# The edge stage of a four-layer graph network: an order written out by hand, loads of five blocks, edges loaded first

## The chip, the cores and the metric

The kernel runs on one NeuronCore of a Trainium2 chip. A core has engines that run side by side, each with its own queue of instructions: TensorE (PE; its weight loads are shown as PEld), VectorE (DVE), ScalarE (ACT), GpSimd (POOL) and SyncE (SP), which here only issues DMAs. DMAs move data between the device's memory (DRAM) and the on-chip memories SBUF and, through an engine, PSUM. An engine takes its instructions in the order of its queue and waits at each one until the data and buffers that it needs are there. The metric is the device time of one execution in microseconds (us), the median of several.

## What is computed

A graph has N = 3125 nodes with 128 features and E = 103125 directed edges (src, dst), sorted by dst. Four graph layers follow one another; each is added to its input and normalised.

```python
x = layernorm(x + relu(segment_sum(edge_weight[:, None] * (x @ W0)[src], dst) + b0))     # layer 0
x = layernorm(x + GAT(x, src, dst))                   # layer 1: attention, 4 heads of 32
x = layernorm(x + (x + edge_softmax(x) @ Wo))         # layer 2: attention with Q, K, V over the edges
x = layernorm(x + sigmoid(SAGE2(relu(SAGE1(x)))))     # layer 3: two mean aggregations
```

The change concerns only what stands before and within layer 0.

## The kernel before

The kernel turns the edge list into two dense tables in DRAM and then works with matrix products. `wd` (3200 x 3200, float32) holds for every pair (node, source) the sum of its edge weights, and `f_ctd` (25 x 128 x 3200, bfloat16) the number of its edges. Nodes are counted in blocks of P = 128, of which there are NB = 25.

**Before the edge stage.** Lines 577 to 642 load dst, src and the weights, compute a sort key of each edge, write a table `td` of keys, local sources and weights to DRAM (L634), and find for each *window* where its edges begin (`row_i`, L641). A window is five nodes (WN = 5); there are NW = 640 windows, in NG = 5 groups of 128. The features x are loaded on SP (L643, L645), and the weights and biases of all layers on ACT's queue (`load`, L541, and L714). Then an indirect DMA a group on GpSimd (L649) fetches 256 edges for each of the group's windows.

**Keys.** `keys_of(g)` (L655 to L695) turns a group's edges so that the edges of a window lie on the partitions, and writes the keys as bfloat16 pairs (`kd2`, `kc2`) and the weight as three bfloat16 parts (`w2`), the third one being also kept in float32 (`wu`). Groups 0 and 1 are done before the stage, the others within it, all at one place (in `make`, at block 8g - 6).

**The edge stage** (L855 to L904) runs over NBT = 40 blocks of BW = 16 windows. For each block

- `make(b)` lets DVE compare keys with a ramp, which gives two one-hot matrices `ohd` and `ohc` (L827), and multiply `ohd` by the weight parts, which gives three `wod` (L836); half of the third is made on ACT (L845), four windows at a time. `make(b + 1)` is called while block b is in work; `ohd`, `ohc` and `wod` have two buffers each.
- For four windows at a time PE makes `cp`, the counts (8 products, L867), and `wp`, the sums of weights (24 products, L875); ACT copies them to `cs` (L880) and `ws` (L886). `cp` and `wp` share three PSUM buffers.
- SP stores `ws` to `wd` (L888), 80 node rows a block, and every second block `cs` to `f_ctd` (L891), 160 node columns.

**Layer 0's products.** `add0` (L787 to L800) loads 128 rows of `wd` by 10 blocks of 128 columns (640 KB, `cw`, three buffers) and multiplies each block by `xw = x @ W0`, summing into five PSUM banks for the first Z0 = 20 blocks of sources (L797). One such product is here called an *add*; the trace has two records for each. There are 25 x 20 = 500 adds. They are queued as soon as the rows that they need have been stored a block earlier. The last five blocks of sources follow after the stage, in other PSUM banks.

What sets the order: nothing is written out by hand in this part. The framework's scheduler fills each engine's queue by readiness and by the order of the code, so adds, copies and key steps move to where it finds room.

Of the kernel before, what the change touches and what calls it, by code (L numbers as in the profile page):

```python
# [7 lines left out]
F32 = mybir.dt.float32  # L8
BF16 = mybir.dt.bfloat16
# [483 lines left out]
BW = 16  # L493
KW = WN * NB
NBT = NW // BW
Z0 = 20
V1 = 100
GA = 80.0
# [10 lines left out]
def fast_path(  # L509
# [28 lines left out]

    def load(name, ap, shape):
        t = cst.tile(shape, F32, name=name)  # L540
        nc.scalar.dma_start(t, ap)  # L541
        return t

    def row(name, v, n):
# [30 lines left out]
    with ExitStack() as st:  # L575
# [64 lines left out]
        nc.vector.tensor_scalar(cnt, cnt, 1.0, 0.0, OP.subtract, OP.max)  # L640
        nc.vector.tensor_scalar(row_i, cnt, float((P * ER - EW) // 16), None, OP.min)  # L641
        nc.vector.tensor_copy(ramp, ramp_i)
    nc.sync.dma_start(x[:, 0:NF, :], x_in[0 : NF * P, :].rearrange("(b p) d -> p b d", p=P))  # L643
    nc.gpsimd.memset(x[:, NF, :], 0.0)
    nc.sync.dma_start(x[0:NR, NF, :], x_in[NF * P : N, :])  # L645
    egs = []
    for g in range(NG):
        eg = ep.tile([P, EW // 16, 3, 16], F32, name="eg", bufs=3)
        nc.gpsimd.indirect_dma_start(  # L649
            out=eg.rearrange("p a t k -> p (a t k)"), out_offset=None, in_=td,  # L650
            in_offset=bass.IndirectOffsetOnAxis(ap=row_i[:, g : g + 1], axis=0),
        )
        egs.append(eg)

    def keys_of(g):  # L655

        eg = egs[g]
        kd2 = kp.tile([P, P // BW, 2, BW, 2], BF16, name="kd2")
        kc2 = kp.tile([P, P // BW, 2, BW, 2], BF16, name="kc2")
        w2 = [kp.tile([P, P // BW, 2, BW, 2], BF16, name=f"w2_{s}") for s in range(3)]  # L660
        kic = ep.tile([P, EW], F32, name="kic", bufs=2)
        nc.vector.tensor_scalar(
            kic.rearrange("p (a k) -> p a k", k=16), eg[:, :, 0, :], thr[:, g : g + 1], None, OP.subtract
        )

        nc.vector.memset(kic[:, EW - 1 : EW], -1.0)
        kid = ep.tile([P, EW], F32, name="kid", bufs=2)
        nc.vector.tensor_copy(kid.rearrange("p (a k) -> p a k", k=16), eg[:, :, 1, :])
        wei = ep.tile([P, EW], F32, name="wei", bufs=2)
        nc.scalar.copy(wei.rearrange("p (a k) -> p a k", k=16), eg[:, :, 2, :])  # L670
        t0 = cps.tile([P, 4, P], F32, name="t0", tag="cw")
        t1 = cps.tile([P, 2, P], F32, name="t1", tag="cw")
        for h in range(2):
            a = slice(h * P, (h + 1) * P)
            nc.tensor.transpose(t0[:, h, :], kid[:, a], ident)
            nc.tensor.transpose(t0[:, 2 + h, :], kic[:, a], ident)
            nc.tensor.transpose(t1[:, h, :], wei[:, a], ident)

        def each(i, h):
            return i[:, h, :].rearrange("p (b w) -> p b w", w=BW)  # L680

        def pairs(i, h):
            return each(i, h)[:, :, :, None].to_broadcast([P, P // BW, BW, 2])

        wt = ep.tile([P, 2, P], F32, name="wt", bufs=2)
        wu = kp.tile([P, 2, P], F32, name="wu")
        for h in range(2):
            copy(kd2[:, :, h, :, :], pairs(t0, h))
            copy(kc2[:, :, h, :, :], pairs(t0[:, 2:, :], h))
            nc.scalar.copy(w2[0][:, :, h, :, :], pairs(t1, h))  # L690
        for s, (i, o) in enumerate(((t1, wt), (wt, wu))):
            for h in range(2):
                nc.vector.tensor_tensor(each(o, h), each(i, h), w2[s][:, :, h, :, 0], OP.subtract)
                nc.scalar.copy(w2[s + 1][:, :, h, :, :], pairs(o, h))
        return kd2, kc2, w2, wu  # L695

    keys = {0: keys_of(0), 1: keys_of(1)}


    l0_wt = load("f_l0_wt", l0_w, [P, P])  # L700
    l0_br = cst.tile([P, P], F32, name="l0_br")
    nc.gpsimd.memset(l0_br, 0.0)
    nc.scalar.dma_start(l0_br[0:1, :], l0_b.rearrange("(o k) -> o k", o=1))
# [7 lines left out]
    nc.gpsimd.memset(att, 0.0)  # L711
    for s, a in enumerate((l1_as, l1_ad)):
        for h in range(H):
            nc.scalar.dma_start(att[h * C : (h + 1) * C, s * H + h : s * H + h + 1], a[h, :].rearrange("(c o) -> c o", o=1))  # L714
    wqt = load("f_wq", l2_wq, [P, P])
    wkt = load("f_wk", l2_wk, [P, P])
    wvt = load("f_wv", l2_wv, [P, P])
# [7 lines left out]
    watt = cst.tile([P, 2 * H], F32, name="watt")  # L725
    wyv = cst.tile([P, 2 * P], F32, name="wyv")
    both = cst.tile([P, P], F32, name="f_both")
    def products_of_weights():
        nc.gpsimd.tensor_tensor(both, gb_row, sb_row, OP.add)
        tw = {}  # L730
        for name, w in (("l1", l1_wt), ("q", wqt), ("k", wkt), ("v", wvt)):
            t = zps.tile([P, P], F32, name="trw", tag="acc3")
            nc.tensor.transpose(t, w, ident)
            tw[name] = ep.tile([P, P], F32, name="tw_" + name)
            nc.scalar.copy(tw[name], t)
        t = zps.tile([P, P], F32, name="trw", tag="acc3")
        nc.tensor.matmul(t[:, 0 : 2 * H], tw["l1"], att, start=True, stop=True)
        nc.scalar.copy(watt, t[:, 0 : 2 * H])
        t = zps.tile([P, P], F32, name="trw", tag="acc3")
        nc.tensor.matmul(t, tw["q"], tw["k"], start=True, stop=True)  # L740
        nc.scalar.copy(wyv[:, 0:P], t)
        t = zps.tile([P, P], F32, name="trw", tag="acc3")
        nc.tensor.matmul(t, tw["v"], wot, start=True, stop=True)
        nc.scalar.copy(wyv[:, P:], t)
# [39 lines left out]
        for j in range(n):  # L784
            nc.tensor.matmul(acc[:, j, :], ones, l0_br, start=(j == 0), stop=False, skip_group_check=True)

    def add0(pool, i, accs, blocks):  # L787

        b0, n = blocks
        for h in range(0, n, 10):  # L790
            m = min(10, n - h)
            cw = pool.tile([P, min(10, n), P], F32, name="cw")[:, 0:m]
            nc.sync.dma_start(
                cw.rearrange("p c d -> p (c d)"), wd[i * P : (i + 1) * P, (b0 + h) * P : (b0 + h + m) * P]
            )
            for j in range(h, h + m):
                nc.tensor.matmul(  # L797
                    accs[j // 4][:, j % 4, :], cw[:, j - h, :], xw[:, i, :], start=False,
                    stop=(i == NB - 1 and (j % 4 == 3 or j == n - 1)), skip_group_check=True,
                )  # L800

    def end0(acc, b0, n):
        t = lp0.tile([P, 4, P], F32, name="r0")
# [2 lines left out]
        )  # L806
        layer_norm(lp0, x[:, b0 : b0 + n, :], t, (0, n), True)

    zp = front.enter_context(tc.tile_pool(name="f_zp", bufs=3))
    sp = front.enter_context(tc.tile_pool(name="f_stg", bufs=2))  # L810
    SB = 2
    wv_ = wd.rearrange("(w i) (c d) -> w (i c) d", i=WN, d=P)

    def make(b):

        if b % 8 == 2 and 8 < b < NBT - 8:
            keys[b // 8 + 1] = keys_of(b // 8 + 1)
        kd2, kc2, w2, w3 = keys[b // 8]
        ohd = op_.tile([P, 2 * BW, P], BF16, name="ohd")
        ohc = op_.tile([P, 2 * BW, P], BF16, name="ohc")  # L820
# [1 line left out]
        def twos(k):  # L822
            k = k[:, b % 8, :, :, :].rearrange("p q w t -> p (q w) t")
            return k[:, :, None, :].to_broadcast([P, 2 * BW, P // 2, 2])

        for o, k in ((ohd, kd2), (ohc, kc2)):
            nc.vector.tensor_tensor(  # L827
                o.rearrange("p w (a t) -> p w a t", t=2), twos(k),
                ramp.rearrange("p (a t) -> p a t", t=2)[:, None, :, :].to_broadcast([P, 2 * BW, P // 2, 2]),
                OP.is_equal,  # L830
            )
        wod = []
        for s in range(3):
            f = of_.tile([P, 2 * BW, P], BF16, name="wod")
            n = 2 * BW if s < 2 else BW
            nc.vector.tensor_tensor(  # L836
                f[:, 0:n].rearrange("p w (a t) -> p w a t", t=2), ohd[:, 0:n].rearrange("p w (a t) -> p w a t", t=2),
                twos(w2[s])[:, 0:n], OP.mult,
            )
            wod.append(f)  # L840

        def more(k):
            for w in range(k, k + 4):
# [4 lines left out]

    cs = None
    acc0 = None  # L850
    done = 0
    cur = make(0)
    for k in range(0, BW, 4):
        cur[3](k)
    for b in range(NBT):  # L855
        ohd, ohc, wod, _ = cur
        cur = make(b + 1) if b + 1 < NBT else None
        if b % SB == 0:
            cs = sp.tile([P, NB, SB * BW * WN], BF16, name="cs")
        ws = sp.tile([P, BW, P], F32, name="ws")  # L860
        for k in range(0, BW, 4):
            cp = cps.tile([P, 4, P], F32, name="cp", tag="cw")
            wp = cps.tile([P, 4, P], F32, name="wp", tag="cw")
            for j in range(4):
# [16 lines left out]
                cs[:, :, i0 : i0 + 4 * WN].rearrange("p c (w i) -> p c w i", i=WN),  # L881
                cp[:, :, 0:KW].rearrange("p w (i c) -> p c w i", c=NB),
            )
            if cur:
                cur[3](k)
            nc.scalar.copy(ws[:, k : k + 4, :], wp)  # L886
        for a, e in ((0, 112), (112, KW)):
            nc.sync.dma_start(wv_[b * BW : (b + 1) * BW, a:e, :].rearrange("w k d -> k w d"), ws[a:e, :, :])  # L888
        if b % SB == SB - 1:
            i0 = (b - SB + 1) * BW * WN  # L890
            nc.sync.dma_start(ctd[:, :, i0 : i0 + SB * BW * WN].rearrange("c d i -> d c i"), cs)  # L891
        if b < 2:
            for blocks in GB[4 * b : 4 * b + 4]:
                xw_of(*blocks)
        if b == 2:
            products_of_weights()
            acc0 = [zps.tile([P, 4, P], F32, name=f"acc{k}", tag=f"acc{k}") for k in range(Z0 // 4)]
            for a in acc0:
                bias0(a, 4)
        while acc0 and (done + 1) * P <= (b - 1) * BW * WN:  # L900
            add0(zp, done, acc0, (0, Z0))
            done += 1
    for i in range(done, NB):
        add0(zp, i, acc0, (0, Z0))  # L904
    front.close()
    r = xw

# [770 lines left out]
```

## Time and profile before

| | us |
|---|---|
| median of 3 runs | 1528.68 (1528.14 to 1530.35) |
| the profiled execution | 1528.75 |
| its span, from the first to the last instruction | 1526.9 |
| busy in the span: PE, DVE, ACT, POOL | 1391.9, 985.8, 910.6, 126.8 |

The stages in the span: up to about 43 us loading, the table and the first keys; to 469 us the edge stage; to 499 us the last adds of layer 0; then the rest of layer 0 and layer 1 to about 970, layer 2 to about 1251 and layer 3 to the end. A busy PE counts the modelled length of pipelined products and so overstates what it works. Shares over the whole span mix these stages; the edge stage has to be read by itself.

In the page's part 2 each digit is the busy share of one fortieth of the span in tenths. The edge stage is slices 1 to 12 there:

```profile
PE   4899999999997987899989989899999999999994
PEld 3898999998997876889979979677777764458994
DVE  4999899999990489879978888544464451012006
ACT  2988778888882479878778677554465431023003
```

### The profile page before, as it was taken

The page shows a single profiled execution, that of the slowest core. Times are in us where ns is not written, and L with a number is a line of the kernel's source. Part 1 is how long each engine was busy: PE and PEld are TensorE (multiplying, and loading weights), DVE is VectorE, ACT ScalarE, POOL GpSimd, SP SyncE. Part 2 cuts the span into 40 slices and gives each one's busy share as a digit, 9 for nine tenths or more (in the row PEclk, how much of TensorE's full clock was granted, in tenths as well). Part 3 has the DMA queues.
Part 4 walks back from the last instruction along what each step waited for, and adds up shares of the span by engine and source line. Part 5 has one row for each costly group of instructions (what it writes and reads, how often), then busy time and mean ns, then how long its engine had stood idle before and what let it go on. Part 6 is the DMA issues. An engine that isn't in the chain of part 4 may idle for free. (4 is left out here: it accounts for less than half of the span.)

```text
span 1526.9 us, 35224 instructions
## 1 busy us (share of the span) xinstructions
PE 1391.9 (91%) x14858; PEld 1220.9 (80%) x14871; DVE 985.8 (65%) x1608; ACT 910.6 (60%) x1865; POOL 126.8 (8%) x162
## 2 busy tenths in 40 slices
PE   4899999999997987899989989899999999999994
PEld 3898999998997876889979979677777764458994
DVE  4999899999990489879978888544464451012006
ACT  2988778888882479878778677554465431023003
POOL 2000000000000023203212311300000000000000
PEclk9999999999998999999999999999999999999997
DMA  6387787887878633444434433332222227503551
GB/s 193 88 216 212 208 228 206 236 211 208 222 211 247 207 96 99 145 123 122 129 121 116 130 89 104 101 111 68 73 64 80 69 89 259 200 22 151 196 174 45
DMA packets 210337, 223.92 MB, mean 147 GB/s; under 512 B 72860, under 2 KB 183975, under 8 KB 209913
## 3 DMA queue, kind: packets, MB, share of 16 engines
q1 hardware_dynamic: 206312, 217.26, 48.4%
q10 hardware_dynamic: 3457, 2.35, 0.6%
q8 instruction: 118, 1.93, 0.5%
q0 software_dynamic: 400, 1.97, 0.4%
q14 instruction: 50, 0.41, 0.1%
HBM read 157.19 MB, written 64.36 MB: 145 GB/s over the span
## 5 line engine op out<-in xcount | busy, mean ns | idle before, releaser
L1244 PE MATMUL acc<-vp,cm 128*128 128x198 bf16 x2500 | 344.5, 252 | 6.6 <-DVE cm L1229 4.1
L1228 ACT ACTIVATE fm<-adr,bas 128x896 bf16<-128x896 f32 (+1 forms) x320 | 286.2, 952 | 67.9 <-DVE cm L1229 63.3
L1239 PE MATMUL acc<-vp,ct 128*128 128x204 bf16 x1250 | 315.2, 256 | 9.7 <-DVE vp L1147 5.6
L1244 PEld LDWEIGHTS <-cm 128*128 128x128 bf16 x2500 | 235.8, 98 | 25.9 <-issue 10.4
L875 PE MATMUL wp<-wod,ohc 128*128 128x128 bf16 x3840 | 244.1, 219 | 8.8 <-ACT cs L880 6.6
L875 PEld LDWEIGHTS <-ohc 128*128 128x128 bf16 x3840 | 224.0, 98 | 9.8 <-issue 9.4
L836 DVE TENSOR_TENSOR wod<-ohd,w 128x4096 bf16<-128x4096 bf16 (+1 forms) x120 | 224.9, 1926 | 0.6 <-PE wp L875 0.6
L1229 DVE TENSOR_TENSOR cm<-fm,ct 128x896 bf16<-128x896 bf16 (+1 forms) x320 | 197.5, 647 | 36.3 <-PE acc L1244 13.2
L845 ACT ACTIVATE wod<-ohd,wu 128x128 bf16<-128x128 bf16 x640 | 197.0, 400 | 0.0
L1384 DVE TENSOR_TENSOR e<-e,ct 128x416 f32<-128x416 f32 (+1 forms) x175 | 108.2, 625 | 106.5 <-ACT e L1383 98.6
L1383 ACT ACTIVATE e<-s,f_nm 128x416 f32<-128x416 f32 (+1 forms) x175 | 109.5, 632 | 98.1 <-PE s L1380 90.8
L1388 PEld LDWEIGHTS acc<-self__8127,e 128*128 128x128 f32 x1250 | 148.4, 193 | 20.6 <-issue 18.8
L1388 PE MATMUL acc<-self__8127,e 128*128 128x129 f32 x1250 | 148.8, 276 | 0.5 <-DVE e L1384 0.5
L1380 PE MATMUL s<-yT,f_xT 128*128 128x416 f32 (+1 forms) x350 | 142.8, 543 | 4.6 <-ACT rt L1360 4.0
L797 PE MATMUL acc<-f_xw,cw 128*128 128x128 f32 x1000 | 119.8, 280 | 7.2 <-DMA cw<-wd 7.2
L1239 PEld LDWEIGHTS <-ct 128*128 128x128 bf16 x1250 | 122.5, 98 | 2.5 <-issue 1.5
L886 ACT COPY ws<-wp 128x512 f32<-128x512 f32 x160 | 93.5, 584 | 49.9 <-PE wp L875 48.3
L797 PEld LDWEIGHTS acc<-f_xw,cw 128*128 128x128 f32 x1000 | 116.3, 196 | 7.5 <-DMA cw<-wd 7.3
L867 PE MATMUL cp<-ohc,ohd 128*128 128x125 bf16 x1280 | 96.8, 218 | 21.0 <-ACT ws L886 17.4
L1380 PEld LDWEIGHTS s<-yT,f_xT 128*128 128x128 f32 x350 | 62.2, 191 | 55.5 <-issue 39.2
L827 DVE TENSOR_TENSOR ohd<-kd,ramp 128x4096 bf16<-128x4096 bf16 x40 | 91.4, 2286 | 21.2 <-PE cp L867 21.1
L1562 PEld LDWEIGHTS <-ct 128*128 128x128 bf16 x1875 | 104.9, 98 | 0.0
(292 smaller groups left out, 1490.3 us busy)
## 6 DMA issues: line engine op xcount, KB each, us to landing
ct<-f_ctd SPq DMA_DIRECT2D x49, 800.0 KB
wd<-ws SPq DMA_DIRECT2D x40, 896.0 KB
ct<-f_ctd SPq DMA_DIRECT2D x150, 224.0 KB
cw<-wd SPq DMA_DIRECT2D x50, 640.0 KB
f_ctd<-cs SPq DMA_DIRECT2D x20, 1000.0 KB
ct<-f_ctd SPq DMA_DIRECT2D x25, 416.0 KB
ct<-f_ctd SPq DMA_DIRECT2D x25, 365.2 KB
cw<-wd SPq DMA_DIRECT2D x25, 320.0 KB
```

The source lines that it names most:

```text
L797: nc.tensor.matmul(accs[j // 4][:, j % 4, :], cw[:, j - h, :], xw[:, i, :], start=False, stop=(i == NB - 1 and (j % 4 == 3 or j == n - 1)) ...
L836: nc.vector.tensor_tensor(f[:, 0:n].rearrange("p w (a t) -> p w a t", t=2), ohd[:, 0:n].rearrange("p w (a t) -> p w a t", t=2), twos(w2[s] ...
L845: nc.scalar.activation(wod[2][:, BW + w, :], ohd[:, BW + w, :], AF.Copy, scale=w3[:, 1, at : at + 1])
L875: nc.tensor.matmul(wp[:, j, :], ohc[:, w, :], wod[s][:, w, :], start=(j == 0 and q == 0 and s == 0), stop=(j == 3 and q == 1 and s == 2), ...
L1228: nc.scalar.activation(f[:, : n * P], at, AF.Relu, bias=bas[:, c, h : h + 1], scale=UP)
L1229: nc.vector.tensor_tensor(m[:, : n * P], f[:, : n * P], ct[:, : n * P], OP.min)
L1239: nc.tensor.matmul(out_(F1, PW), ct[:, k * P : (k + 1) * P], vp[:, c, hp : hp + 2, :, 2 * F1 : V1], start=(c == 0), stop=False, skip_group ...
L1244: nc.tensor.matmul(out_(0, 2 * F1)[:, j], ms[j][:, k * P : (k + 1) * P], vp[:, c, hp + j, :, 0 : 2 * F1], start=False, stop=(c == NB - 1 a ...
L1380: nc.tensor.matmul(s[:, :m], xT[:, c * P : (c + 1) * P], yT[:, i0 * P + a : i0 * P + a + m], start=True, stop=True)
L1383: nc.scalar.activation(e[:, a : a + m], s[:, :m], AF.Exp, bias=nm[:, q : q + 1], scale=scale)
L1384: nc.vector.tensor_tensor(e[:, a : a + m], e[:, a : a + m], ct[:, a : a + m], OP.mult)
L1388: nc.tensor.matmul(acc[k // 3][:, (k % 3) * (P + 1) : (k % 3 + 1) * (P + 1)], es[q, c][:, k * P : (k + 1) * P], vo[:, c, 0 : P + 1], start ...
```

## The change

It does the following.

- The last block has 4 windows instead of 16 (LW = 4): 628 windows are the first to cover 3125 nodes. The 60 rows of `wd` that no window writes any more are set to zero by six stores from a tile `none`, and the end of the last `cs` by a memset.
- Until the table `td` is stored, only edges (and layer 0's weight and bias) are loaded. x is loaded behind the second indirect DMA, and all other weights behind x, on SP's queue instead of ACT's.
- `keys_of` becomes `key_steps`, seven steps. For group 0 they run at once; those of group g + 1 run in the blocks 8g to 8g + 6, one a block. The turned keys go from PSUM to SBUF first (`k_`, `w_`).
- From block 3 on, the order of PE, DVE, ACT and SP is that of the code (`manual_schedule`). After each four windows 3 or 4 adds from a list follow.
- `adds5` loads 5 blocks of columns at a time (320 KB, ZB = 6 buffers). A block's loads are issued behind its own stores of `ws`, for rows that were stored a block earlier, and its store of `cs` behind the loads.

```diff
+LW = 4
+NL = (NBT - 1) * BW + LW
+Z5 = 5
+ZB = 6
...
     def load(name, ap, shape):
         t = cst.tile(shape, F32, name=name)
-        nc.scalar.dma_start(t, ap)
+        with tc.issue_after(x_load.ins):
+            nc.sync.dma_start(t, ap)
         return t
...
-    nc.sync.dma_start(x[:, 0:NF, :], x_in[0 : NF * P, :].rearrange("(b p) d -> p b d", p=P))
-    nc.gpsimd.memset(x[:, NF, :], 0.0)
-    nc.sync.dma_start(x[0:NR, NF, :], x_in[NF * P : N, :])
...
+        if g == 1:
+
+            with tc.issue_after(got.ins):
+                nc.gpsimd.memset(x[:, 0:1, 0:1], 0.0)
+                nc.gpsimd.memset(x[:, NF, :], 0.0)
+    x_load = nc.sync.dma_start(x[:, 0:NF, :], x_in[0 : NF * P, :].rearrange("(b p) d -> p b d", p=P))
...
+        def turn():
+            t = cps.tile([P, 4, P], F32, name="t", tag="cw")
+            for h in range(2):
+                nc.tensor.transpose(t[:, h, :], kid[:, h * P : (h + 1) * P], ident)
+                nc.tensor.transpose(t[:, 2 + h, :], kic[:, h * P : (h + 1) * P], ident)
+            nc.scalar.copy(k_, t)
...
+        def twice():
+            for h in range(2):
+                nc.scalar.copy(kd2[:, :, h, :, :], pairs(k_, h))
+                nc.vector.tensor_copy(kc2[:, :, h, :, :], pairs(k_[:, 2:, :], h))
+                nc.scalar.copy(w2[0][:, :, h, :, :], pairs(w_, h))
...
+        return [
+            columns, turn, twice, lambda: less(0, w_, wt), lambda: part(1, wt), lambda: less(1, wt, wu),
+            lambda: part(2, wu),
+        ]
...
+    def adds5(k):
+
+        i, h = divmod(k, Z0 // Z5)
+        cw = zp.tile([P, Z5, P], F32, name="cw")
+        nc.sync.dma_start(
+            cw.rearrange("p c d -> p (c d)"), wd[i * P : (i + 1) * P, h * Z5 * P : (h + 1) * Z5 * P]
+        )
+        return [
+            lambda j=j: nc.tensor.matmul(
+                acc0[(h * Z5 + j) // 4][:, (h * Z5 + j) % 4, :], cw[:, j, :], xw[:, i, :], start=False,
+                stop=(i == NB - 1 and (h * Z5 + j) % 4 == 3), skip_group_check=True,
+            )
+            for j in range(Z5)
+        ]
...
-    zp = front.enter_context(tc.tile_pool(name="f_zp", bufs=3))
+    zp = front.enter_context(tc.tile_pool(name="f_zp", bufs=ZB))
...
     for b in range(NBT):
+        if b == 3:
+
+            order = ExitStack()
+            order.enter_context(
+                tc.manual_schedule(
+                    engines={mybir.EngineType.PE, mybir.EngineType.DVE, mybir.EngineType.Activation, mybir.EngineType.SP}
+                )
+            )
         ohd, ohc, wod, _ = cur
         cur = make(b + 1) if b + 1 < NBT else None
+        nw = BW if b < NBT - 1 else LW
+        if b % 8 == 0 and b < NBT - 8:
+            steps = key_steps(b // 8 + 1)
+        at = b % 8 if b < NBT - 8 else 7
...
             nc.scalar.copy(ws[:, k : k + 4, :], wp)
+            m = min(4 if k == 4 else 3, len(todo))
+            for f in todo[:m]:
+                f()
+            del todo[:m]
+            added += m
+            if k == 4 and at in (1, 2, 4, 6):
+                steps[{1: 1, 2: 2, 4: 4, 6: 6}[at]]()
...
-        if b % SB == SB - 1:
-            i0 = (b - SB + 1) * BW * WN
-            nc.sync.dma_start(ctd[:, :, i0 : i0 + SB * BW * WN].rearrange("c d i -> d c i"), cs)
...
-        while acc0 and (done + 1) * P <= (b - 1) * BW * WN:
-            add0(zp, done, acc0, (0, Z0))
-            done += 1
-    for i in range(done, NB):
-        add0(zp, i, acc0, (0, Z0))
+
+        while b > 2 and (loads // (Z0 // Z5) + 1) * P <= b * BW * WN and loads < added // Z5 + ZB:
+            todo += adds5(loads)
+            loads += 1
+        if b % SB == SB - 1:
+            i0 = (b - SB + 1) * BW * WN
+            nc.sync.dma_start(ctd[:, :, i0 : i0 + SB * BW * WN].rearrange("c d i -> d c i"), cs)
+    order.close()
+    for f in todo:
+        f()
+    while loads < NB * Z0 // Z5:
+        for f in adds5(loads):
+            f()
+        loads += 1
```

## The prediction

> **What bounds the kernel now.** I read the windows view first, cut at the borders of the edge stage, because shares over the whole span mix five stages. Block 3's last copy out of PSUM ends at 84.5 us and block 39's last edge product at 468.9.
>
> ```profile
> core 0: us, PE busy (x) PEld busy (x) DVE busy (x) ACT busy (x) POOL busy (x), PEclk, DMA share, GB/s
> 84.50:469.00 384.50, 358.91 (x5444) 353.70 (x5441) 354.48 (x204) 317.99 (x875) 0.05 (x1) 1.00 0.81 216
> 469.00:499.20 30.20, 22.44 (x170) 21.93 (x170) 3.71 (x23) 2.25 (x4) 1.40 (x2) 0.83 0.71 212
> 0.00:43.27 43.27, 19.62 (x116) 17.23 (x117) 22.38 (x47) 15.98 (x45) 7.68 (x19) 1.00 0.58 171
> 43.27:84.50 41.23, 36.98 (x571) 35.34 (x571) 41.23 (x21) 38.43 (x111) 0.00 (x0) 1.00 0.50 133
> ```
>
> In the long row PE (359 us) and DVE (354) are both near the stage's 384, ACT is at 318 and the DMA engines at 0.81: there is no single bound, and each engine idles some 25 to 30 us, by turns. The waits view of that stretch says on whom.
>
> ```profile
> PE cp L867 <- ACT ws L886: 17.4, 12, 1.6
> ...
> DVE ohd L827 <- PE cp L867: 21.1, 16, 1.7
> ```
>
> No product waits for a DMA there. Then the timeline, for the price of one step and for the tail (start, duration, engine, operation).
>
> ```profile
> 436.60 0.60 PE L867 MATMUL cp<-ohc,ohd 128*128 128x125 bf16 x8
> ...
> 438.38 0.60 PE L867 MATMUL cp<-ohc,ohd 128*128 128x125 bf16 x8
> ...
> 470.74 9.30 PE L797 MATMUL acc<-f_xw,cw 128*128 128x128 f32 x80
> 473.59 3.23 SPq L888 DMA_DIRECT2D wd<-ws  x2
> 476.87 1.57 SPq L891 DMA_DIRECT2D f_ctd<-cs  x1
> 478.55 22.81 SPq L793 DMA_DIRECT2D cw<-wd  x9
> ...
> 487.19 11.92 PE L797 MATMUL acc<-f_xw,cw 128*128 128x128 f32 x80 [7.16 <-DMA cw<-wd]
> ```
>
> Four windows (8 cp and 24 wp products) take 438.38 - 436.60 = 1.78 us. 80 records are 40 adds of a 128x128 block, so one add is about 9.1/40 = 0.226 us. DVE's five operations of a block repeat every 9.94 us when nothing stops them (ohd at 440.88, the next at 450.82). The tail shows PE standing 7.16 us for a load.
>
> Last the DMA queue, in windows in which it moved one kind each: a store of wd, a store of f_ctd, loads of cw.
>
> ```profile
> DMA packets 2004, 1.02 MB, mean 237 GB/s; under 512 B 87, under 2 KB 2003, under 8 KB 2003
> ...
> DMA packets 3165, 1.02 MB, mean 204 GB/s; under 512 B 3098, under 2 KB 3165, under 8 KB 3165
> ...
> DMA packets 371, 1.23 MB, mean 350 GB/s; under 512 B 30, under 2 KB 143, under 8 KB 371
> ```
>
> So wd takes about 4 us of the queue per block, f_ctd 5 us per two blocks, and a load of 320 KB 0.95 us.
>
> **What the Trainium skill says.** "DMA: Bandwidth & Descriptors", section Queues, rings and completion order: on one issuing engine's ring, descriptors are consumed in order. The trace agrees: in the tail the load issued at 478.55 released PE only at 487.19, behind a wd and an f_ctd store. Same page, Issuing engines are not separate DMA queues: moving an issue from ACT to SP saves issue time only; before, a weight's issue costs ACT 0.44 us (the row at 8.71). "TensorE: Matmul & The Clock Gate", section HAM oscillation: PE gaps over about 3.4 us while a DMA is awaited bring the clock back to half. The trace agrees: after the 7.16 us gap 80 records took 11.92 us instead of 9.30, at a mean clock of 0.83.
>
> **The change, part by part.**
>
> *Twelve windows fewer.* Block 39 has 4 windows of 16: PE saves 3 x 1.78 = 5.3 us, DVE about 7 of its 9.94. Six stores of zeros (0.77 MB, some 3 us of queue) replace them early, beside compute: nothing.
>
> *Fixed order.* From block 4 each group of 4 windows carries 3 or 4 adds, 13 a block. PE per block: 4 x 1.78 + 13 x 0.226 = 10.06 us. DVE: 9.94 plus about 2.4 us of keys per 8 blocks = 10.24. ACT: four times (cs 0.47, four scalings 1.29, ws 0.47) = 8.9, with keys 9.5. The slots fit. Blocks 4 to 39 need of PE 35 x 7.12 + 1.78 + 449 adds x 0.226 + 3 key turns x 1.3 = 356 us, where before took 384. I leave 3 us for frictions: -25 us. With frictions as before (28) it would be 0; with none -28.
>
> *Loads behind the stores.* I followed the code's counters, which the instruction order of the changed program confirms on PE and SP. A load of row i is queued at the end of the first block b with 128(i+1) <= 80b, after block b's own wd store, and its adds stand in PE's queue in the order of the loads. 80 node rows a block bring 12.5 adds, 13 are spent, so the list runs dry. The first load of a batch is then used in the first slot of the next block (loads 0, 44, 52, 60, 64, 72, 80, 84), in the second (24, 32, 40) or in the third (4, 12, 20, 48, 68, 76, 88).
> PE ends block b at B. The last ws copy ends at B + 0.5 (cs, scalings and ws stand on ACT behind the last cp). The load lands L after that store's issue. L from the tail: 487.19 - 473.59 = 13.6, less 5.0 for the f_ctd store between them, less 0.95 because that load was twice as large: 7.7. Landing B + 8.2. PE reaches the first slot's adds at B + 1.8, the second's at B + 4.25, the third's at B + 6.9. Waits: 8 x 6.4 = 51, 3 x 4.0 = 12, 7 x 1.3 = 9, in all 72 us. Later loads of a batch land 0.95 us apart and five adds last 1.1 us, so they wait for nothing more. Before, the scheduler put adds where the data was there. Queued behind the waiting add on PE are the next cp and wp; ACT waits for those, and DVE, one block ahead, waits for cp. PE and DVE are equally loaded, so the wait is lost for both; only where DVE is late anyway is some of it covered. I take 66 (bounds 30, if L were 5 us, and 80, if the f_ctd store of the block before still fills the queue).
>
> *The clock after such a wait.* 8 waits of over 3.4 us; the trace's one example cost 11.92 - 9.30 = 2.6 us. 8 x 2.6 = 21; I take 16 (bounds 0 and 28, the latter with the 4 us waits).
>
> *Key steps.* The same operations in seven places, with two more copies on ACT (k_ and w_, some 1 us a group, in its 9.5); DVE's 2.4 us a group is in the sum. PE's turn is 12 records, 1.3 us, in the sum. The groups' stalls of before (three of 3 us) are in the 25.
>
> *Start.* Before, the table's store at 13.6 shared the queue with x, which lands at 19.39, and the first gather started at 23.27. Without x and weights I put the gather at 17.5, and DVE's first make is some 6 us earlier. But ACT was busy 38.4 of 41.2 us in blocks 0 to 3 already, and all of f_xw's 14 copies (0.5 us each) and group 1's first key copies now fall there, some 50 us of ACT work after the first keys at about 31. Block 3 ends at about 82 instead of 84.5: -2.5 (bounds +4 and -8). SP's 26 weight loads and six stores of zeros go ahead of the first wd store: 34 issues x 0.44 = 15 us from 20, before that store is ready at 45: nothing; if they ran late, ACT's third ws would wait, 5 us at most.
>
> *Tail.* From the last edge product, the quarter store, three loads (2.9), the last f_ctd store (5.1), five loads (4.8) and the landing come to about 20, with the last adds 21, where before took 30.2: -9 (bounds -4 and -13). What follows has the same instruction order as before on all engines: 0.
>
> Sum: -25 + 66 + 16 - 2.5 - 9 = +45.5 us. The profiled execution took 1528.75 us (span 1526.9), practically the median 1528.68: 1528.7 + 45 = **1574 us**.
>
> **The rivals.** *Faster: the loads are hidden.* If DVE paces the stage (10.24 us a block against PE's 10.06) and PE reaches the first slot late, or a load lands within 2 us of its slot, no wait is left: -25 - 2.5 - 9 = -37, 1492 us. For it: today's queue is free for a fifth of the time and no load holds PE within the stage. Against: those adds were placed when the data was there. It decides where waits and clock together stay below 37 us, a mean first-slot wait under about 3.5 us. *Half-hidden:* loads 3 us sooner: 8 x 3.5 + 3 = 31 of waits, clock 6: 1529, between 1513 and 1545. *Worse:* each wait also lets the f_ctd store of the pair collide with the next batch, and every wait over 3.4 us costs the clock two periods: waits 80, clock 28: 1600. That the change does not do what it says is excluded by the instruction order: the adds stand where the code puts them.
>
> **How the numbers follow.** Likeliest, as summed, 0.63 (own range 1548 to 1594); hidden 0.16; half-hidden 0.13; worse 0.08. The range reaches down to 1500 into the hidden case, up to 1594, and leaves out some 0.11 below and 0.06 above. About 0.2% is what a measurement of this kernel can tell from no change. Faster: 0.16 + 0.05 = 0.21; same 0.03; slower 0.76.
>
> **What would show it.** In the profile after, the add's line should have idle time before it released by "DMA cw<-wd", some 60 to 70 us in about 11 long waits, most of them from block 20 on; PEclk under 1.0 in the second half of the stage; the stage from block 4 to 39 near 441 us; the gather before 19 us; the tail near 21 us. No such idle time, and a stage under 365 us, would prove the forecast wrong; waits of 2 to 3 us would mean that L was mis-sized.

## The result and the profile after

The changed kernel takes 1582.63 us (median of 4, 1581.79 to 1582.88) where the kernel before, beside it on the same chip, takes 1529.07 (1528.14 to 1530.35): a ratio of 1.0351, 95% interval 1.0339 to 1.0363. It is 3.5% slower, 8.6 us above the forecast of 1574 and within its range.

From the page of the changed kernel: its span, the busy times, and the group of the adds (busy us, mean ns of one, then the idle time of the engine ahead of them and what ended it).

```profile
span 1581.1 us, 35138 instructions
...
PE 1410.5 (89%) x14775; PEld 1238.9 (78%) x14775; DVE 980.0 (62%) x1613; ACT 912.8 (58%) x1857; POOL 141.3 (9%) x164
...
L857 PE MATMUL acc<-f_xw,cw 128*128 128x128 f32 x1000 | 155.3, 298 | 67.0 <-DMA cw<-wd 66.8
```

The same group on the page of the kernel before:

```profile
L797 PE MATMUL acc<-f_xw,cw 128*128 128x128 f32 x1000 | 119.8, 280 | 7.2 <-DMA cw<-wd 7.2
```

The adds have 67 us of idle PE ahead of them instead of 7, all but 0.2 of it ended by a load of `wd`. The windows view of the changed kernel, cut near the end of block 3 and at 531.5, about one us before the last edge product ends (the columns are those of the prediction's first fence), says where:

```profile
36.07:88.00 51.93, 47.22 (x639) 44.57 (x638) 45.00 (x31) 48.10 (x138) 13.79 (x2) 1.00 0.46 120
88.00:531.50 443.50, 383.52 (x5388) 377.76 (x5386) 347.48 (x208) 319.44 (x868) 1.35 (x1) 0.93 0.74 191
531.50:556.00 24.50, 17.09 (x139) 16.52 (x136) 4.06 (x25) 3.09 (x6) 1.45 (x2) 0.86 0.84 226
```

The long stretch grew from 384.5 to 443.5 us. PE is busy for 384 of them, the DMA engines are less busy than before (0.74 instead of 0.81), and the granted clock is 0.93 instead of 1.00. The waits view of the stretch from 88 to 532 us (us in total, times, longest):

```profile
ACT cs L972 <- PE cp L959: 115.2, 113, 7.9
DVE ohd L895 <- PE cp L959: 86.3, 29, 8.6
PEld acc L857 <- DMA cw<-wd: 63.2, 18, 7.3
PE acc L857 <- DMA cw<-wd: 59.8, 17, 7.1
```

ACT and DVE wait for PE, and PE waits for the load. One such wait in the timeline, at the end of a block:

```profile
289.90 0.60 PE L959 MATMUL cp<-ohc,ohd 128*128 128x125 bf16 x8
290.34 1.50 PE L967 MATMUL wp<-wod,ohc 128*128 128x128 bf16 x24
290.51 3.21 SPq L987 DMA_DIRECT2D wd<-ws  x2
293.83 2.21 SPq L853 DMA_DIRECT2D cw<-wd  x4
297.68 1.65 PE L857 MATMUL acc<-f_xw,cw 128*128 128x128 f32 x6 [5.83 <-DMA cw<-wd]
299.11 1.05 PE L959 MATMUL cp<-ohc,ohd 128*128 128x125 bf16 x8
299.95 2.09 PE L967 MATMUL wp<-wod,ohc 128*128 128x128 bf16 x24
```

The block's store of `ws` is issued at 290.51, the loads behind it from 293.83 on, and the adds of the next block's first slot start at 297.68 (a slot is the products of four windows and the adds behind them; a block has four). PE has done that slot's products at about 291.8 and stands for 5.83 us. After the wait the same 8 and 24 products take 1.05 and 2.09 us instead of 0.60 and 1.50, for the clock is at half until 301.2.

The difference, taken at the ends of PE's products (so that the stretches add up):

| | before | after | difference |
|---|---|---|---|
| last product of block 3 | 82.9 | 87.0 | +4.1 |
| from there to the last edge product | 385.9 | 445.6 | +59.7 |
| from there to the last add of the tail | 30.3 | 22.9 | -7.4 |
| the rest | 1027.8 | 1025.6 | -2.2 |
| span | 1526.9 | 1581.1 | +54.2 |

### The profile page after: what moved, and what is told of

It reads as the page before. It is cut to its first block, busy times and chain, and to the rows that moved or that the text cites. A ratio compares the mean times of both kernels' runs of the same rounds, so it can differ in the third digit from the quotient of the medians.

```text
span 1581.1 us, 35138 instructions
## 1 busy us (share of the span) xinstructions
PE 1410.5 (89%) x14775; PEld 1238.9 (78%) x14775; DVE 980.0 (62%) x1613; ACT 912.8 (58%) x1857; POOL 141.3 (9%) x164
## 5 line engine op out<-in xcount | busy, mean ns | idle before, releaser
L967 PE MATMUL wp<-wod,ohc 128*128 128x128 bf16 x3768 | 247.4, 224 | 1.8 <-ACT k__328 L699 1.6
L967 PEld LDWEIGHTS <-ohc 128*128 128x128 bf16 x3768 | 228.1, 101 | 2.6 <-issue 2.0
L906 DVE TENSOR_TENSOR wod<-ohd,w 128x4096 bf16<-128x4096 bf16 (+2 forms) x122 | 221.1, 1868 | 0.0
L857 PE MATMUL acc<-f_xw,cw 128*128 128x128 f32 x1000 | 155.3, 298 | 67.0 <-DMA cw<-wd 66.8
L857 PEld LDWEIGHTS acc<-f_xw,cw 128*128 128x128 f32 x1000 | 132.7, 204 | 70.6 <-DMA cw<-wd 70.6
L972 ACT CAST cs<-cp 128x500 bf16<-128x500 f32 x157 | 90.5, 577 | 118.9 <-PE cp L959 118.6
L895 DVE TENSOR_TENSOR ohd<-kd,ramp 128x4096 bf16<-128x4096 bf16 (+1 forms) x41 | 90.1, 2200 | 89.5 <-PE cp L959 89.4
L1667 PE MATMUL acc<-ip,ct 128*128 128x128 bf16 x1800 | 104.3, 219 | 0.0
```

Of the source, the lines that this page charges most:

```text
L857: lambda j=j: nc.tensor.matmul(acc0[(h * Z5 + j) // 4][:, (h * Z5 + j) % 4, :], cw[:, j, :], xw[:, i, :], start=False, stop=(i == NB - 1 a ...
L906: made = nc.vector.tensor_tensor(packed(f, ww), packed(ohd, ww), twos(w2[s])[:, ww], OP.mult)
L967: nc.tensor.matmul(wp[:, j, :], ohc[:, w, :], wod[s][:, w, :], start=(j == 0 and q == 0 and s == 0), stop=(j == 3 and q == 1 and s == 2), ...
L1667: nc.tensor.matmul(acc[g][:, j, :], ct[:, (b0 + j) * P : (b0 + j + 1) * P], ups[b // 4][:, b % 4, s, :], start=(b == 0 and s == 0 and j == ...
```

## The experiments

### Adds two block ends behind their loads

```diff
-ZB = 6
+ZB = 7
...
-            m = min(4 if k == 4 else 3, len(todo))
+            m = min(4 if k == 4 else 3, sum(a <= b - 2 for a in since))
...
             todo += adds5(loads)
+            since += 5 * [b]
```

> Only the place of the adds in PE's order is changed: an add is taken from the list no sooner than two block ends after its load was queued (and a seventh buffer, so that the list does not run dry). Theory of the prediction (the loads land after the adds that stand first in PE's queue): the adds' line loses its idle time on DMA cw<-wd between 88 and 532 us, from 60 to under 8, the half clock goes with it, and 13 adds more are left for the tail (+3 us). Stage some 375 us, total 1583 - 60 - 18 + 3 = about 1508 us (1495 to 1525). Rival, the fixed order itself is slow: the idle time of PE moves to waits for DVE and ACT, total over 1560 us. Rival, the DMA queue is short of room: the adds wait all the same, total over 1555 us.

Measured: 1498.25 us, ratio to before 0.9808 (0.9788 to 0.9828). The windows view of this run, with the waits of PE and DVE in the long stretch:

```profile
86.50:444.60 358.10, 357.11 (x5380) 354.64 (x5378) 345.63 (x208) 317.83 (x868) 1.35 (x1) 1.00 0.91 236
```

```profile
ACT cs L973 <- PE cp L960: 31.9, 95, 0.8
...
DVE ohd L895 <- PE cp L960: 3.3, 7, 1.1
```

No add waits for a load any more, PE idles 1.0 of 358 us at full clock, and the DMA engines are busy for 0.91 of the time. Nothing but the place of the adds and a buffer was changed, and the slower kernel became one about 2% faster than before. Both rivals are excluded by that: PE isn't held up by the order written by hand, and the queue isn't short. The stage, 358 us in this view, came out shorter than the expected 375.

### The buffer alone

```diff
-ZB = 6
+ZB = 7
```

> The changed kernel with seven buffers for the loads instead of six, nothing else: the control for the runs that have seven buffers and a delay of the adds. Theory (the place of the adds does it, not the buffers): the same first-slot waits, about 60 us in the stage, total 1583, within 4 us. Rival, a load that waits for a buffer is the cause: waits fall by 15 us or more, total below 1570.

Measured: 1582.77 us, ratio 1.0362 (1.0346 to 1.0379), and 59.3 us of waits for `cw` in the stage. The seventh buffer alone does nothing; the delay does it.

### The order left to the scheduler

```diff
-        if b == 3:
-            order = ExitStack()
-            order.enter_context(tc.manual_schedule(
...
-    order.close()
```

> Only the fixed order is taken out: the scheduler fills the queues again, with the loads of five blocks, the key steps and all else as after the change. Theory of the prediction: adds are placed where the data is there, waits on cw<-wd under 20 us in the stage, total 1500 to 1535 us. Rival, the waits come from the place of the loads behind the stores and not from the order on PE: waits of 40 us or more remain and the total is over 1555 us.

Measured: 1518.36 us, ratio 0.9929 (0.9912 to 0.9945). The waits view of PE from block 3 to the last edge product lists no load:

```profile
PE wp L959 <- ACT cs L964: 7.2, 10, 1.3
PE cp L951 <- ACT ws L970: 4.3, 6, 1.6
PE wp L959 <- ACT ws L970: 3.0, 3, 1.4
```

The scheduler puts the adds where the data is there, as the theory has it, and pays 14.5 us in waits between PE and ACT in their place. The stage takes 378.7 us from product to product, 19.6 more than with the fixed order and delayed adds (359.1); the other 5 us stay open.

### Loads half a block earlier, adds at once

```diff
+            while k == 8 and b > 2 and (loads // (Z0 // Z5) + 1) * P <= b * BW * WN and loads < added // Z5 + ZB:
+                todo += adds5(loads)
+                loads += 1
...
-        while b > 2 and (loads // (Z0 // Z5) + 1) * P <= b * BW * WN and loads < added // Z5 + ZB:
-            todo += adds5(loads)
-            loads += 1
```

> Only the place of the loads in SP's queue is changed: the loads that stood behind a block's own stores of ws are queued half a block earlier, ahead of them; the adds still follow at once. Theory of the prediction (the add meets a load that lands 6 us too late): the long waits become waits of 1 to 3 us[...], PEclk 0.98 or more, total some 1583 - 40 = about 1540 us (1515 to 1560). Rival, a shortage of the DMA queue: the stores behind the loads come later by as much, and the total stays within 10 us of 1583. Rival, the fixed order itself is slow: same.

Measured: 1524.71 us, ratio to before 0.9971 (0.9959 to 0.9984). The total is in the range, but the waits have another shape than expected: six in the stage, 18.2 us in all, the longest 4.8; and the clock in the stage is 0.97, not 0.98 or more, for the four of 2.82 us and longer each have a half-clock stretch with them. The timeline of this run shows why some waits stay:

```profile
411.56 2.03 SPq L990 DMA_DIRECT2D wd<-ws  x2
413.63 1.70 SPq L1001 DMA_DIRECT2D f_ctd<-cs  x1
419.00 3.13 SPq L853 DMA_DIRECT2D cw<-wd  x4
...
420.70 0.66 PE L857 MATMUL acc<-f_xw,cw 128*128 128x128 f32 x4
424.18 0.80 PE L857 MATMUL acc<-f_xw,cw 128*128 128x128 f32 x2 [2.82 <-DMA cw<-wd]
```

SP has nothing else to issue from 415.3 on, but the loads are issued at 419.00: they read rows of the store issued at 411.56, and SP stands until that has landed, 7.4 us after its issue. By SP's own waits view such loads waited for a store 22 times in this stage, 54.5 us in all. The Trainium skill, "DMA: Bandwidth & Descriptors", section Two DMAs through the same engine are not ordered, says that a load of what a store wrote has to wait for that store's completion; this is that wait. The load's own way of 5 us follows. So moving the issue ahead only exchanges the wait behind the block's own store for one on the store before.

### Loads half a block earlier, adds a block later

This joins the edit just shown (with `since` kept beside `todo`, as in the first run) and a delay of one block, with ZB = 7:

```diff
+            m = min(4 if k == 4 else 3, sum(a < b for a in since))
```

> The loads stand ahead of the block's own stores of ws in SP's queue, and an add is taken from the list no sooner than in the block after its load was queued (seven buffers). Each load then has the best part of a block between its landing and its add. Theory of the prediction: no wait on cw<-wd in the stage, stage as with the two block ends of delay (359 us), but 51 adds instead of 64 left for the tail and the last loads earlier, so 1498 - 3 to -6 = about 1494 us (1488 to 1501). Rival, the stores behind the loads come late and hold ACT's ws copies (two buffers): stage 365 us or more, total over 1502 us.

Measured: 1505.65 us, ratio 0.9841 (0.9828 to 0.9855): above the expected range, and not for the rival's reason. ACT's `ws` copies wait for 1.3 us only (from 90 to 450 us), and for PE, not for a store; four waits for loads are left, 5.5 us in all. One of them:

```profile
421.41 2.01 SPq L993 DMA_DIRECT2D wd<-ws  x2
...
426.97 4.57 SPq L853 DMA_DIRECT2D cw<-wd  x4
...
434.12 1.46 PE L857 MATMUL acc<-f_xw,cw 128*128 128x128 f32 x6 [1.87 <-DMA cw<-wd]
435.37 1.05 PE L960 MATMUL cp<-ohc,ohd 128*128 128x125 bf16 x8
```

The load is issued 5.6 us after the store of 421.41, and its add can run 12.7 us after that store's issue, in the next block's first slot. So with the loads half a block earlier the delay to the next block is still too little by about 2 us; two block ends behind the loads, as in the first run, were enough. The wait of 1.87 us was also enough for the clock: the 8 products behind it take 1.05 us instead of 0.60.

### The store of f_ctd ahead of the loads

In the changed kernel the two are exchanged at the end of each odd block:

```diff
+        if b % SB == SB - 1:
+            i0 = (b - SB + 1) * BW * WN
+            nc.sync.dma_start(ctd[:, :, i0 : i0 + SB * BW * WN].rearrange("c d i -> d c i"), cs)
         while b > 2 and (loads // (Z0 // Z5) + 1) * P <= b * BW * WN and loads < added // Z5 + ZB:
...
-        if b % SB == SB - 1:
```

> The changed kernel with the store of f_ctd (each second block) put ahead of the loads instead of behind them; nothing else. Theory of the prediction (a load lands when what stands ahead of it in SP's queue is through): the batches queued at odd block ends land some 5 us later. Three of the first-slot waits (loads 0, 52, 72), one second-slot (32) and four third-slot ones (12, 48, 68, 88) grow by 4 to 5 us each, +32 to 38 us, and the clock costs some 10 us more; total about 1583 + 42 = 1625 us (1605 to 1640). Rival, the wait is a fixed latency of the load or of the rows' own stores, whatever stands between: within 8 us of 1583.

Measured: 1638.66 us, ratio to before 1.072 (1.0703 to 1.0736); the waits in the stage are 100.0 us instead of 59.8. The timeline at the end of block 23, whose batch is that of load 52:

```profile
355.03 1.58 SPq L987 DMA_DIRECT2D wd<-ws  x1
356.66 1.61 SPq L998 DMA_DIRECT2D f_ctd<-cs  x1
358.38 6.42 SPq L853 DMA_DIRECT2D cw<-wd  x4
...
366.50 1.22 PE L857 MATMUL acc<-f_xw,cw 128*128 128x128 f32 x4 [9.99 <-DMA cw<-wd]
```

Without the exchange this wait is 5.18 us. The other two first-slot waits behind odd blocks grew from 7.08 to 12.09 and from 5.17 to 9.96 us; those behind even blocks stayed (5.83 and 6.12, 5.22 and 5.31, 6.59 and 6.41). The total came out inside the expected range of 1605 to 1640. What stands ahead of a load in SP's queue is what its add pays for; a wait that is the same whatever stands between is excluded.

### The last block with 16 windows

```diff
-LW = 4
+LW = 16
```

> The changed kernel with 16 windows in the last block again, so that nothing is stored as zero rows; nothing else. Theory: three more steps of four windows on PE (5.3 us) or DVE's longer make (7 us) come back on the path; but 10 more adds find room in these slots, which shortens the tail by up to 2 us: total 1583 + 5 = about 1588 us (1584 to 1591). Rival, the tail is set by the last store and the loads behind it, which also move with the block: +7 to +9. Rival, hidden: no change.

Measured: 1590.44 us, ratio to before 1.0394 (1.0378 to 1.041), 7.8 us above the changed kernel. Between products the stage is longer by 10.6 us (456.2), of which 5.3 are the products and 2.3 the ten more adds at the forecast's prices, and 1.6 more waiting; the tail is shorter by 1.2 us, as the theory has it. So leaving out twelve windows is worth about 8 us here. That can't be told from the 5.3 of the sum: by the two intervals the difference lies between some 2 and 11 us, and it fits the rival's 7 to 9 as well.

### The start

Four runs, one in the changed kernel and three in faster variants. The first undoes the start alone:

```diff
-        with tc.issue_after(x_load.ins):
-            nc.sync.dma_start(t, ap)
+        nc.scalar.dma_start(t, ap)
...
-        if g == 1:
-
-            with tc.issue_after(got.ins):
```

> Only the start is undone: x is loaded ahead of the gathers and the weights on ACT's queue, as before the change. Theory: the late x holds PE and ACT in blocks 0 to 3 for more than the earlier gather brings; block 3 ends near 84 us instead of 88 and the total falls by 2 to 5 us, to about 1579. Rival: the six us that the earlier gather gave to DVE are worth more; the total rises by 3 to 6 us.

Measured: 1582.56 us, ratio to before 1.0348 (1.033 to 1.0366): no difference to the changed kernel, so that neither the theory nor its rival came true. Block 3's last product ends at 87.1 us instead of 87.0, though the gather starts at 23.91 again. The second goes with the loads half a block earlier and the adds a block later, and besides undoes the start and makes `f_xw` ahead of the blocks:

```diff
+    for blocks in GB:
+        xw_of(*blocks)
     cur = make(0)
...
-        if b < 2:
-            for blocks in GB[4 * b : 4 * b + 4]:
-                xw_of(*blocks)
```

> As the run with the loads ahead of the stores and adds a block later, and besides the start as before the change (x ahead of the gathers, weights on ACT's queue) with all of f_xw made ahead of block 0 instead of in blocks 0 and 1. Theory that ACT's work within blocks 0 to 3 sets where block 3 ends: 7.7 us of copies leave the stretch, the gather comes 4 us later; block 3 ends near 83 us instead of 86 and the total is 2 to 4 us below the other run. Rival, DVE's makes set it: block 3 ends at 88 or later, the total is 2 to 4 us above.

Measured: 1505.29 us, ratio 0.9841 (0.9828 to 0.9855), no difference from the 1505.65 without it, and again neither reading came true. Block 1 took 11.7 us instead of 16.3, as wanted, but block 0 ended at 55.9 instead of 47.0, and block 3 at 87.7 instead of 86.3. The last two start from the fastest version (the next part) and issue x behind the first gather:

```diff
-        if g == 1:
+        if g == 0:
```

> As the run with the last f_ctd store behind the last loads, but x is loaded behind the first gather instead of the second. Theory of the start (x lands at 34 us, so all 14 copies of f_xw fall into ACT's queue in blocks 0 and 1, where block 1 takes 16 us instead of 10.5): x lands some 5 us sooner, part of the copies is done before block 0, block 3 ends 2 to 4 us sooner, total about 1494 (1492 to 1496). Rival, ACT's work is the same wherever it stands: within 1.5 us of 1496.6.

> As the run with x behind the first gather, with f_xw made ahead of block 0 in the code instead of in blocks 0 and 1. Theory of the start: no f_xw copy stands between the copies of cs and ws any more; block 1 takes 11.6 us instead of 16, block 0 ends later by less than that; block 3 ends 2 to 5 us sooner than 86.3, total about 1493 (1491 to 1496). Rival, block 0 loses what block 1 gains: within 1.5 us of 1496.6, or slower.

Measured: 1496.14 us (0.9786, 0.9772 to 0.98) and, with `f_xw` first, 1497.88 (0.9795, 0.9782 to 0.9808), beside 1496.58 without either edit: no difference that could be told. Block 3's last product ended at 87.6 and 87.4 us, PE waited for x until 33.9 and 33.6 us as it did before these edits (33.5), so that the earlier landing on which the theory rested did not come, and block 0 lost what block 1 gained. The rival's reading fits both.

### The last store of f_ctd behind the last loads

With the adds two block ends behind, as in the first run, and

```diff
-        if b % SB == SB - 1:
+        if b % SB == SB - 1 and b < NBT - 1:
...
         loads += 1
+    i0 = (NBT - SB) * BW * WN
+    nc.sync.dma_start(ctd[:, :, i0 : i0 + SB * BW * WN].rearrange("c d i -> d c i"), cs)
     front.close()
```

> As the run with adds two block ends behind their loads, and besides the last store of f_ctd is queued behind the last loads of layer 0 instead of between them. Theory: the tail is set by what stands ahead of the last loads in SP's queue, so some 4 to 5 us of store leave it: tail 20 to 21 us instead of 24.8, total about 1494 us (1491 to 1497). Rival, the last loads wait for their rows' store, and the f_ctd store runs beside it: within 1.5 us of 1498. Rival, layer 1 then waits for f_ctd: no gain or a loss.

Measured: 1496.58 us, ratio to before 0.979 (0.9776 to 0.9803). The tail in the windows view, of the first run:

```profile
444.60:469.50 24.90, 19.52 (x144) 18.65 (x143) 3.75 (x24) 2.32 (x4) 1.45 (x2) 0.86 0.86 229
```

and of this one:

```profile
445.50:465.10 19.60, 16.64 (x144) 16.06 (x143) 3.60 (x21) 2.24 (x4) 1.45 (x2) 1.00 1.04 286
```

The tail lost 5.3 us as expected, its half clock with them; what follows it took 2.4 us more (1029.7 instead of 1027.3), so that of the expected 4 us some 2 remain, less than the intervals of the two runs can tell apart. By the total, theory and rivals can't be told apart either; the tail speaks for the theory. For the 2.4 us one thing is on record: a half-clock stretch of 6.8 us from 468.1 on, just behind the tail, where the first run has one of 3.4 us from 473.5 on. By its median this version is among the fastest, 2.1% below the kernel before.

## Why the prediction was right

The main step held: the adds stand in PE's queue ahead of the data, and the lost time is the waits and the clock behind them. That the number came within 8.6 us is in part luck, since terms that were off by 6 us and more cancelled. By the sum's terms:

| term | forecast | what the runs showed |
|---|---|---|
| fixed order and fewer windows | -25 | about -24 |
| waits for loads | +66 | +59.8 |
| half clock behind them | +16 | some +22 to +24 |
| start | -2.5 | +4.1 |
| tail | -9 | -7.4 |
| what follows | 0 | -2.2 |

*Fixed order.* The run with delayed adds shows this term bare: 359.1 us from the last product of block 3 to the last edge product where before took 385.9, that is -26.8. It does 13 adds fewer there than the forecast counted (436 instead of 449, 2.9 us at the forecast's 0.226 each), which leaves -24. PE is the bound, as the count of 356 us took it, for it idles 1.0 us. So the 3 us left for frictions were no idle time; they covered an add that was priced too low. A slot of that run:

```profile
300.38 0.60 PE L960 MATMUL cp<-ohc,ohd 128*128 128x125 bf16 x8
...
302.16 0.89 PE L857 MATMUL acc<-f_xw,cw 128*128 128x128 f32 x6
302.89 0.60 PE L960 MATMUL cp<-ohc,ohd 128*128 128x125 bf16 x8
```

With three adds (six records) it takes 2.51 us instead of 1.78, so an add costs 0.24 us, and at that price the forecast's own count for 436 adds comes to 359.5.

*Waits.* The eight first-slot waits were priced 8 x 6.4 = 51 and measured 46.6 (5.15 to 7.08); the three second-slot ones 12 and 8.7 (2.65 to 3.14); the third-slot ones 9 and 4.6, in six that the view lists. The list of loads 0, 44, 52, 60, 64, 72, 80, 84 came true one by one, so reading the counters of the code was enough to place each wait. The forecast's L was 7.7 us from a store's issue to the load's landing behind it; the example above has 297.68 - 290.51 = 7.2. "Hidden" failed on that, for it needed a mean first-slot wait under about 3.5 us, and "half-hidden" counted on 3.5; the mean was 5.8.

*Clock.* This term was too small. The stage is 445.6 - 359.1 = 86.5 us longer than with delayed adds; less 59.8 of waits and 2.9 for the 13 adds, 23.8 remain for the clock and small frictions. The windows view of the changed kernel around the example shows one piece:

```profile
297.70:301.20 3.50, 3.50 (x26) 3.44 (x27) 1.07 (x3) 1.00 (x3) 0.00 (x0) 0.50 0.48 175
301.20:305.00 3.80, 3.80 (x59) 3.79 (x56) 0.00 (x0) 2.86 (x9) 0.00 (x0) 1.00 0.00 0
```

At half clock for 3.5 us PE loses 1.75 us. The clock's records in the trace show eleven half-clock stretches in the stage, one with each of the eleven waits of 2.65 us and more; the part of each that lies behind its wait costs 22 us in all, 2.0 apiece. The forecast had 2.6 apiece, but for eight waits only, and took 16 of the 21: it let only waits over 3.4 us count. The three of 2.65 to 3.14 us counted too.

*Start.* This term has the wrong sign. The gather started at 19.61 us (17.5 forecast, 23.27 before), and DVE's make for block 1 began at 37.21 instead of 43.19, six us earlier as forecast. But that lead was lost in block 1, which took 16.2 us between its products where before took 10.5. DVE's part of the timeline of the changed kernel there:

```profile
60.62 0.49 DVE L708 COPY kc<-k__328 128x256 bf16<-128x256 bf16 x2 [2.76 <-ACT k__328 L699]
62.61 2.29 DVE L895 TENSOR_TENSOR ohd<-kd,ramp 128x4096 bf16<-128x4096 bf16 x1 [1.50 <-PE cp L959]
```

DVE waits for the new key copy `k_` on ACT, then for PE. Before, DVE's makes followed one another without a gap from 43.19 on. ACT was busy for 48.1 of 51.9 us in this stretch. The forecast had named that ACT was nearly full and then still let the lead of six us outweigh it. But the late x isn't the whole of it: in the run that undoes the start DVE's make for block 1 begins at 43.81, about where it began before the change, and block 3 still ends at 87.1 and not at 82.9. What that run keeps of the change, the key steps in the blocks and their copies `k_` and `w_` among it, costs some 4 us there even without the late x; which of it does was not separated, and four attempts to move x or the copies of `f_xw` left the total where it was. The size is rough as well: seven other runs with the same start and the order fixed from block 3 on have block 3's end between 85.5 and 86.5 us. (The border of 84.5 that the prediction calls the end of block 3's last copy before is its start; it ends at 85.1. The table above goes by products.)

*Tail.* 22.9 us instead of 21. The last wait, of 5.53 us, has a half-clock stretch with it (clock 0.86), of which the 4.5 us behind the wait cost 2.3 us.

Of the signs named: the adds' line has its 67.0 us (60 to 70 were named; 7.0 of them lie in the tail), the long waits in the stage are eleven, seven of them from block 20 on, the stage is 443.5 us in the row above (441), and the clock is 0.93; the gather, at 19.61, was later than 19, and the tail, at 22.9, longer than 21. The forecast was 8.6 us low: the start (6.6) and the clock (6 to 8) were too low by more than that, and the waits, too high by 6, took most of the difference back.

## What to carry to other kernels

An order written by hand is as good as its weakest distance: ask of each instruction that waits for a DMA what stands ahead of that DMA in its queue, and put the use behind its landing. Here the stage lost some 84 us for adds one block end too near to their loads, and the delay of a second block end, with one buffer more, returned all of it. A wait on PE, which bounds this stage, was paid twice: 60 us as idle time and 22 to 24 as clock.

## What the runs showed of the hardware beyond that

PE's clock went to half with waits as short as 1.87 and 2.22 us in a stage in which PE was otherwise busy (the run with loads half a block earlier and adds a block later). The Trainium skill, "TensorE: Matmul & The Clock Gate", section HAM oscillation: how this bites in real kernels, gives the rule as no idle gaps of PE over about 3.4 us. The effect is the one that it describes, but these runs show it with shorter waits than that. The length alone doesn't decide it: a wait of 2.05 us in the run with adds at once, and one of 2.78 in the run with the store of `f_ctd` ahead, have no half clock with them. In the clock's records of the runs with these waits the half-clock stretches of the stage are 3.4, 6.8 or 10.2 us long, so that the clock can be down for longer than the wait was.

And a store of a block's `ws` takes its time until its rows can be used: in the two timelines above a load that depends on it was issued 5.6 and 7.4 us after the store, and the add behind that load ran 7.2 and 5.2 us later, in both some 12.6 us from the issue of the store to the use of its rows (421.41 to 434.12, 411.56 to 424.18).
